# An entry of the experts' token lists becomes 64 bytes instead of 4

## The chip, the cores and the metric

The kernel runs on one core of one Trainium2 chip. The metric is the device time of one execution in microseconds, lower being better; the time shown for a kernel is the median of several executions. A core has five engines with a queue of instructions each: TensorE (PE in the profile; its weight loads are PEld), VectorE (DVE), ScalarE (ACT), GpSimd (POOL) and SyncE (SP, which only issues DMAs). POOL issues the indirect DMAs, whose rows are picked by a list of indices. An engine runs its queue in order: an instruction that waits holds up all behind it.

## The reference, cut to what matters

The model has two layers on x of shape (4, 512, 512), all in float32. The first is a cumulative cross-attention and a feed-forward layer with Hadamard transforms. The second is a softmax attention over 1024 context rows a batch, and then a mixture of experts, which is the stage in question:

```python
router_logits = x2d @ gate_kernel                       # 2048 tokens, 32 experts
routing_weights = softmax(router_logits)
routing_weights, selected_experts = top_k(routing_weights, 8)
routing_weights = routing_weights / sum(routing_weights)
...                                                     # the tokens of each expert, sorted
inter = silu(tokens @ gate_proj[e]) * (tokens @ up_proj[e])   # 512 -> 192
expert_out = inter @ down_proj[e]                             # 192 -> 512
output[token] = sum over its 8 experts of weight * expert_out
x = x + output
```

2048 tokens with 8 experts each make 16384 pairs of token and expert.

## The kernel before, in words

**Before the experts.** Up to 725 us of the profiled execution the kernel does the first layer and loads; from 725 to about 1055 us it goes over the 16 tiles of 128 tokens (loop `for step in range(NTT)`), and each step holds a stage of several tiles: scores, read-out, router (`choose`) and `place_rows`.

**The lists.** `il_d` is a list in DRAM: each expert has a stretch of LS = 2320 entries of one int32, an entry being a token's number. Entries never written hold a number past the last token, put there early by `blank_rows` (L120 to 134). `place_rows(t)` (L1063 to 1092) counts, on TensorE and DVE, which place in its experts' stretches each token of tile t gets, writes the eight places into `slots`, and then POOL issues eight indirect DMAs (L1082), one for each of a token's eight experts: 128 words of 4 bytes, each to its own place in `il_d`. There are 128 of these scatters.

**Early experts.** Six experts (EARLY) start on the tokens of the first 11 tiles. `start_early` (L1094) reads two column tiles of their lists at once; `early_rows` gathers their token rows into the wide buffers big2, big0, big1, big3 (experts 0 to 3) and two smaller tiles (4, 5); their steps are T (transposes), G (the products of gate and up) and D_ (down), put between the last steps of the attention by an order written out by hand for PE, DVE and ACT. D_ writes its results over the gathered rows, and `early_adds` has POOL add them to the output in DRAM.

**The loop over all experts.** After the lists are complete, the 32 experts are gone through by size ("rank"); their tile counts and tile heights are fixed (FIXED: 7 tiles of 126 tokens, six of 128, and so on to 2 of 100). An expert with more than four tiles is worked in two *parts*: 14 of the 32 are (one of 7 tiles, five of 6, eight of 5). The order is the three largest, then the largest left, each of the next five behind one of the small ones, so that among experts 0 to 31 of the loop numbers 3, 5, 7, 9 and 11 are small. For each expert:

- `load_list` (L1426): SP reads the expert's entries from `il_d` into `ids`, five experts ahead; eight `ids` tiles rotate. `read_lists` (L911) makes each such read wait for all scatters.
- `load_rows` (L1435): POOL gathers the token rows by these numbers, one DMA a tile (`gather`, L903), three experts ahead, into one of three `xg` tiles. It is called by `turned`, when the last part of the expert three before has been transposed; that expert's weight sums (`weights_of`, L1410), which read the same tile, must be done too.
- `turn` (L1346 and following): TensorE transposes the rows; ACT and DVE copy them out of PSUM (L1164, L1166).
- `gate_up` (L1361): three products on TensorE (L1373) through two PSUM tiles; ACT does the Silu of the first (L1173), DVE multiplies it with the second (L1174), and the third product, the rest of gate and up, goes into the first one's PSUM tile.
- `output` (L1447): `down` on TensorE (L1188, L1191); `finish` scales each result tile by the routing weight and writes it to `y`, even tiles on ACT (L1200), odd ones on DVE (L1198); then `add_rows` (L1384) has POOL issue one indirect DMA a tile that adds y's rows to the output in DRAM (L1387). `tc.issue_after(gathers[-1])` puts these adds behind the gathers traced last in POOL's queue. The adds of one expert wait until those of the expert before have landed, since both may add to the same token's row.

TensorE works ahead: the transposes of the next part stand between this part's gate-up and down. `y` has tag "y" in a pool of three buffers, taken in turn by each part.

A dynamic loop after that (L1548 and following) takes the tokens that a fixed size had no room for.

Of the kernel before, what the change touches and what calls it, by code (L numbers as in the profile page):

```python
# [9 lines left out]
F32 = mybir.dt.float32  # L10
I32 = mybir.dt.int32
# [7 lines left out]
P = 128  # L19
# [4 lines left out]
EARLY = 6  # L24
ER = 2
# [8 lines left out]
    + [(3, 128), (3, 117), (3, 108), (3, 100)] + [(2, 112), (2, 100)]  # L34
)
SPARE = 1024


def most_extra(tokens: int, experts: int) -> int:
# [9 lines left out]
def kernel(  # L49
# [26 lines left out]
    nc = tc.nc  # L76
    B, S, D = x.shape
# [3 lines left out]
    NT = B * S  # L81
# [5 lines left out]
    NX = most_extra(NT, E)  # L87

    LS = NT + 272
    IL = -(-(E * LS + P) // SPARE) * SPARE  # L90

    XW = D + E

# [10 lines left out]
    xn_d = dram.tile([NT + SPARE, XW], F32, name="xn_d")  # L104
    xa_d = dram.tile([CUT * P + P, XW], F32, name="xa_d")

    il_d = dram.tile([IL, 1], I32, name="il_d")

    xe_d = dram.tile([1, NX], I32, name="xe_d")
    xi_d = dram.tile([P, NX], I32, name="xi_d")  # L110
# [11 lines left out]
    def blank_rows():  # L122


        room = x_sb[:, NTT - TPB :, :].rearrange("p t d -> p (t d)")
        zeros = room[:, :XW]
        nc.gpsimd.memset(zeros, 0.0)
        fill = room[: IL // SPARE, SPARE : 2 * SPARE].bitcast(I32)
        nc.gpsimd.iota(fill, pattern=[[1, SPARE]], base=NT, channel_multiplier=0)
        for i in range(SPARE // P):  # L130
            rows = slice(NT + i * P, NT + (i + 1) * P)
            nc.sync.dma_start(out=xn_d[rows, :], in_=zeros)
        nc.sync.dma_start(out=xa_d[CUT * P :, :], in_=zeros)
        nc.sync.dma_start(out=il_d.rearrange("(p f) o -> p (f o)", f=SPARE), in_=fill)

    def load_x(b):
        return nc.sync.dma_start(
# [765 lines left out]
    def gather(xg, src, idx, rows):  # L903
        ins = nc.gpsimd.indirect_dma_start(  # L904
            out=xg,
            out_offset=None,
            in_=src[:, :],
            in_offset=bass.IndirectOffsetOnAxis(ap=idx, axis=0),
            bounds_check=rows - 1,
            oob_is_err=False,  # L910
        ).ins  # L911
        gathers.append(ins)
        return ins

    def read_lists(dst, src):
        ins = nc.sync.dma_start(out=dst, in_=src).ins
        for s in scatters:
            tc.add_manual_dep(
                ins, s.name,
                mybir.DependencyInfo(mybir.DependencyClass.Sync, mybir.DependencyReason.DATA),  # L920
                reason="lists written",
            )
# [13 lines left out]
    with tc.tile_pool(name="ctx2", bufs=1) as ctx2, tc.tile_pool(  # L936
# [127 lines left out]
        def place_rows(t):  # L1064

            nonlocal run
            sel = chosen.pop(t)
            ps = ps_o.tile([P, 512], F32, tag="o", name="o")
            nc.tensor.matmul(ps[:, :E], upper, sel, start=True, stop=False)
            nc.tensor.matmul(ps[:, :E], ones, run, start=False, stop=True)  # L1070
            nxt = aw.tile([P, E], F32, tag="run", name="run")
            nc.vector.tensor_add(nxt, run, sel)
            run = nxt

            val = aw.tile([P, E], F32, tag="val", name="val")
            nc.vector.tensor_mul(val, ps[:, :E], sel)
            slot1 = small.tile([P, K], F32, tag="slot1", name="slot1")
            nc.vector.max(slot1, val)
            nc.vector.tensor_scalar_add(slots[:, t * K : (t + 1) * K], slot1, -1.0)
            for k in range(K):  # L1080
                j = t * K + k
                ins = nc.gpsimd.indirect_dma_start(  # L1082
                    out=il_d[:, :],
                    out_offset=bass.IndirectOffsetOnAxis(ap=slots[:, j : j + 1], axis=0),
                    in_=tok[:, t : t + 1],
                    in_offset=None,
                    bounds_check=IL - 1,
                    oob_is_err=False,
                ).ins
                if scatters:  # L1090
                    tc.declare_no_dep(ins, group="rows", reason="rows of different pairs")
                tc.add_to_no_dep_group("rows", ins)
                scatters.append(ins)

        def start_early():

            nonlocal run
            ps = ps_o.tile([P, 512], F32, tag="o", name="o")
            nc.tensor.matmul(ps[:, :E], ones, run, start=True, stop=True)
            nxt = aw.tile([P, E], F32, tag="run", name="run")  # L1100
            nc.vector.tensor_tensor(nxt, ps[:, :E], early1, ALU.max)
            run = aw.tile([P, E], F32, tag="run", name="run")
            nc.vector.tensor_scalar_mul(run, nxt, 1.0 / P)
            ids = route_p.tile([P, EARLY, ER], I32, name="ids")
            read_lists(
                ids,
                il_d[: EARLY * LS, :]
                .rearrange("(e n) o -> e n o", n=LS)[:, : ER * P, :]
                .rearrange("e (p c) o -> p e (c o)", c=ER),
            )  # L1110
            near = route_p.tile([P, EARLY, ER], I32, name="near")
            nc.vector.tensor_scalar_min(near, ids, float(CUT * P))
            early.extend((ids[:, e, :], near[:, e, :]) for e in range(EARLY))
# [188 lines left out]
    with tc.tile_pool(name="rw", bufs=1, reuse_waits="tile") as rw, tc.tile_pool(  # L1302
# [81 lines left out]
        def add_rows(y, idx):  # L1384


            ins = nc.gpsimd.indirect_dma_start(  # L1387
                out=of[:, :],
                out_offset=bass.IndirectOffsetOnAxis(ap=idx, axis=0),
                in_=y,  # L1390
                in_offset=None,
                bounds_check=NT - 1,
                oob_is_err=False,
                compute_op=ALU.add,
            ).ins
            group = f"adds{len(adds)}"
            if adds[-1]:
                tc.declare_no_dep(ins, group=group, reason="rows of different tokens")
            tc.add_to_no_dep_group(group, ins)
            for s in adds[-2]:  # L1400
                tc.add_manual_dep(
                    ins, s.name,
                    mybir.DependencyInfo(
                        mybir.DependencyClass.Sync, mybir.DependencyReason.DATA
                    ),
                    reason="sums of the rows before",
                )
            adds[-1].append(ins)
# [11 lines left out]
        class Fixed:  # L1420
# [5 lines left out]
            def load_list(self):  # L1426
                nt, q = self.nt, self.q
                at = number(start_i, self.r, (E - 1) * LS)
                self.ids = er.tile([P, TM], I32, tag="ids", name="ids", bufs=8)
                read_lists(  # L1430
                    self.ids[:q, :nt],
                    il_d[bass.ds(at, nt * q), :].rearrange("(p c) o -> p (c o)", c=nt),
                )

            def load_rows(self):  # L1435
                nt, q = self.nt, self.q
                self.xg = er.tile([P, TM, XW], F32, tag="xg", name="xg")
                for c in range(nt):
                    gather(self.xg[:q, c, :], xn_d, self.ids[:q, c : c + 1], NT + SPARE)

            def load_weights(self):
                self.wt = fetch(number(order_i, self.r, E - 1))
# [4 lines left out]
        def output(x, t0, nt, h1, h2, w):  # L1447
            q = x.q
            ps = down(h1, h2, nt, q, x.wt[1], x.wt[2])
            y = er.tile([P, 4, D], F32, tag="y", name="y")  # L1450
            for i in range(nt):
                finish(i, ps[i][:q, :D], y[:q, i, :], w[:q, t0 + i : t0 + i + 1])
            with tc.issue_after(gathers[-1]):
                for i in range(nt):
                    add_rows(y[:q, i, :], x.ids[:q, t0 + i : t0 + i + 1])


        large, little = list(range(26)), [30, 28, 27, 26, 29]
# [89 lines left out]
        with tc.If(nx > 0):  # L1548
# [59 lines left out]
            with tc.For_i(0, nx, 1) as i:  # L1608
                one = bass.ds(i, 1)
                e_t = er.tile([1, 1], I32, tag="e_t", name="e_t", bufs=1)  # L1610
                nc.sync.dma_start(out=e_t, in_=xe_d[:, one])
                row = er.tile([P, 1], I32, tag="row", name="row", bufs=1)
                nc.sync.dma_start(out=row, in_=xi_d[:, one])
                hot_t = er.tile([P, E], F32, tag="hot", name="hot", bufs=1)
                nc.sync.dma_start(
                    out=hot_t, in_=hot_d[one, :].rearrange("o e -> (o e)").partition_broadcast(P)
                )
                ids = er.tile([P, 1], I32, tag="ids1", name="ids1", bufs=1)
                gather(ids, il_d, row, IL)
                e = nc.sync.value_load(e_t[0:1, 0:1], min_val=0, max_val=E - 1)  # L1620
                x = Fixed(0, 1, P)
                x.wt, x.ids = fetch(e), ids
                x.xg = er.tile([P, TM, XW], F32, tag="xg", name="xg")
                gather(x.xg[:, 0, :], xn_d, ids, NT + SPARE)
                hs = gate_up(x.wt[0], turn(x.xg, 0, 1, P), 1, P)
                output(x, 0, 1, *hs[:2], weights_of(x.xg, hot_t, 1, P))
                adds.append([])
# [70 lines left out]
```

## Time and profile before

| | us |
|---|---|
| median of 3 executions | 1713.23 (1712.88 to 1713.24) |
| profiled execution, device time | 1729.91 |
| its span, from first to last instruction | 1728.1 |
| PE busy in the span | 1653.4 |
| POOL busy in the span | 597.1 |
| adds of y on POOL, 141 | 224.7 |
| gathers of token rows on POOL, 141 | 151.5 |
| scatters into the lists on POOL, 128 | 126.5 |

The profile is of one execution. A row of the timeline gives the start in us from the span's start, the time it took, engine, line, operation, output and inputs by the program's names with shapes, a count, and in brackets how long the engine had been idle before it and what ended that. Lines are those of the kernel before. In the chain of waits a row is a start, a time and what the end of the program was waiting for then; "issue" is time in which nothing that the profile shows was waited for. A row for a stretch of time gives its length, the busy time of PE, PEld, DVE, ACT and POOL with their instruction counts, the granted TensorE clock (1.00 is full), the share of the DMA engines' time and what they moved in GB/s. A row of the costliest groups gives busy time, mean ns of one, and the idle time just before them.

### The profile page before, as it was taken

To read this page: it belongs to the slowest core of one execution; us is meant where nothing else is said; L and a number is where in the kernel's file an instruction comes from. 1 tells how busy PE (TensorE), PEld (TensorE's weight loads), DVE (VectorE), ACT (ScalarE), POOL (GpSimd) and SP (SyncE) were. 2 spreads that over 40 slices of the span, in tenths; PEclk is the share of its full clock that TensorE was granted. 3 is DMA by queue.
4 is the path that set the end of the run, shared out by engine and by line. 5 is a ranking of instruction groups with operands and counts; after the bars stand their busy time and mean duration, and the time that the engine had idled before them with its cause. 6 is when DMAs were issued, how large, how long until landed. Compare 5 with 4: busy or idle time off the path is not lost.

```text
span 1728.1 us, 17728 instructions
## 1 busy us (share of the span) xinstructions
PE 1653.4 (96%) x6050; PEld 1010.0 (58%) x6050; DVE 764.7 (44%) x1715; ACT 509.7 (29%) x854; POOL 597.1 (35%) x522
## 2 busy tenths in 40 slices
PE   7999999999999999999999968999999999999996
PEld 3685657776766777545545445555555666544443
DVE  4693457755785445444434325223222323232332
ACT  2510333322332111145656522222222222222221
POOL 1000120101000100103444555657565675456664
PEclk9999999999999999999999988999999999999998
DMA  9314110000000000354431236979677887668774
GB/s 346 125 49 122 49 63 27 1 1 1 1 1 5 20 0 1 123 197 113 100 87 51 58 51 111 242 128 208 153 158 165 201 181 161 146 174 185 180 158 64
DMA packets 92718, 181.76 MB, mean 105 GB/s; under 512 B 23906, under 2 KB 24546, under 8 KB 92625
## 3 DMA queue, kind: packets, MB, share of 16 engines
q0 software_dynamic: 40560, 73.04, 23.3%
q1 hardware_dynamic: 51198, 106.72, 19.6%
q8 instruction: 48, 0.79, 0.2%
q10 hardware_dynamic: 866, 0.85, 0.2%
q14 instruction: 46, 0.37, 0.1%
HBM read 132.38 MB, written 51.62 MB: 106 GB/s over the span
## 4 chain that ended last, share of the span: by engine, by line
PE 82%; issue 5%; DMA 4%; DVE 4%; POOL 2%; ACT 2%; ACTq 0%; POOLq 0%; DVEq 0%; SPq 0%
PE g L1373 19%; PE q L717 17%; PE dn L364 11%; PE dn L1188 6%; PE o L1018 6%; PE sc L988 6%; PE gu L342 5%; PE dn L1191 4%; PE tr L1354 3%; DMA out_dram<-y,ids 2%; POOL il_d L1082 2%; PE tr L167 1%; DMA x_sb<-in_cn_dram 1%; PE gu L332 1%; PE o L1038 1%
## 5 line engine op out<-in xcount | busy, mean ns | idle before, releaser
L1373 PE MATMUL g<-xgt,gu 128*128 128x360 f32 (+24 forms) x1104 | 346.0, 470 | 0.0
L1373 PEld LDWEIGHTS g<-xgt,gu 128*128 128x128 f32 x1104 | 204.9, 190 | 149.9 <-issue 77.4
L1387 POOL DMA_INDIRECT out_dram<-y,ids x141 | 224.7, 1593 | 107.6 <-issue 39.1
L364 PE MATMUL dn<-wdn,h 128*128 128x512 f32 x448 | 200.3, 593 | 0.0
L904 POOL DMA_INDIRECT xg<-xn_d,ids x141 | 151.5, 1074 | 129.7 <-issue 107.9
L1082 POOL DMA_INDIRECT il_d<-tok,slots x128 | 126.5, 988 | 197.7 <-DVE sel L1052 70.9
L717 PE MATMUL q<-big,s 128*128 128x256 f32 x768 | 173.6, 379 | 0.0
L717 PEld LDWEIGHTS q<-big,s 128*128 128x128 f32 x768 | 145.9, 190 | 19.8
L1188 PE MATMUL dn<-d,h 128*126 128x512 f32 (+8 forms) x306 | 150.0, 600 | 0.0
L364 PEld LDWEIGHTS dn<-wdn,h 128*128 128x128 f32 x448 | 84.1, 190 | 92.8 <-issue 91.6
L717 PE MATMUL q<-big,wgu 128*128 128x256 f32 x576 | 132.4, 379 | 0.0
L1174 DVE TENSOR_TENSOR h<-g,sg 128x256 f32<-128x256 f32 (+25 forms) x52 | 27.0, 519 | 222.4 <-PE g L1373 204.9
L717 PEld LDWEIGHTS q<-big,wgu 128*128 128x128 f32 x576 | 109.3, 190 | 25.7 <-issue 9.3
L342 PE MATMUL gu<-big,wgu 128*128 128x256 f32 x512 | 117.9, 388 | 3.3 <-ACT sg L349 3.3
L1018 PE MATMUL o<-big,pt 128*128 128x512 f32 x256 | 116.4, 603 | 3.8 <-issue 2.6
L988 PE MATMUL sc<-big,qt 128*128 128x512 f32 x256 | 114.1, 599 | 0.3 <-ACT qt L170 0.3
L342 PEld LDWEIGHTS gu<-big,wgu 128*128 128x128 f32 x512 | 98.4, 194 | 26.8 <-issue 7.6
L374 POOL TENSOR_TENSOR x_sb<-x_sb,y 128x512 f32<-128x512 f32 x16 | 19.9, 1271 | 258.3 <-DVE y L373 258.3
L278 POOL TENSOR_TENSOR x_sb<-x_sb,beta_t 128x512 f32<-128x512 f32 x16 | 23.7, 1504 | 235.2 <-ACT y L267 222.7
L1200 ACT ACTIVATE y<-dn,w 126x512 f32<-126x512 f32 (+8 forms) x82 | 56.3, 687 | 139.2 <-PE dn L1191 134.5
L731 ACT ACTIVATE sg<-q,wsu_t 128x256 f32<-128x256 f32 x96 | 45.4, 473 | 171.5 <-DVE q L753 84.0
L1354 PEld LDWEIGHTS tr<-ident,xg 126*128 126x128 f32 (+8 forms) x564 | 64.9, 142 | 53.3 <-issue 19.1
(244 smaller groups left out, 1969.7 us busy)
## 6 DMA issues: line engine op xcount, KB each, us to landing
gu<-in_w_gu_dram SPq DMA_DIRECT2D x38, 768.0 KB
big<-in_cn_dram SPq DMA_DIRECT2D x10, 1024.0 KB
d<-in_w_dn_dram SPq DMA_DIRECT2D x38, 256.0 KB
big<-in_ct_dram SPq DMA_DIRECT2D x8, 1024.0 KB
x_sb<-in_cn_dram SPq DMA_DIRECT2D x12, 512.0 KB
d<-in_w_dn_dram SPq DMA_DIRECT2D x38, 128.0 KB
xn_d<-xr SPq DMA_DIRECT2D x16, 272.0 KB
x_sb<-in_x_dram SPq DMA_DIRECT2D x4, 1024.0 KB
```

The source lines that it names most:

```text
L342: nc.tensor.matmul(ps[:, :n], wt[:, c, fs], xhs[b][:, c, cols], start=(c == 0), stop=(c == DC - 1),)
L364: nc.tensor.matmul(ps[:, :D], h[:, i * P : (i + 1) * P], wdn[:, fc, :], start=(fc == 0), stop=(fc == FC - 1),)
L717: nc.tensor.matmul(q[:, m * HS : (m + 1) * HS], w[:, m, k, :], x[:, k, :], start=(k == 0), stop=(k == 1),)
L904: ins = nc.gpsimd.indirect_dma_start(out=xg, out_offset=None, in_=src[:, :], in_offset=bass.IndirectOffsetOnAxis(ap=idx, axis=0), bounds_c ...
L988: nc.tensor.matmul(ps[:, bass.ts(h, M // 2)], qt[:, c, :], keys[b][h][:, c, :], start=(c == 0), stop=(c == DC - 1),)
L1018: nc.tensor.matmul(ps[:, :D], pt[:, c, :], values[b][c // (MC // 2)][:, c % (MC // 2), :], start=(c == 0), stop=(c == MC - 1),)
L1082: ins = nc.gpsimd.indirect_dma_start(out=il_d[:, :], out_offset=bass.IndirectOffsetOnAxis(ap=slots[:, j : j + 1], axis=0), in_=tok[:, t : ...
L1188: nc.tensor.matmul(p[:q, :D], h1[:, bass.ts(i, q)], d1, start=True, stop=False)
L1191: nc.tensor.matmul(p[:q, :D], h2[half, bass.ts(i, q)], d2[half, :], start=False, stop=True)
L1354: nc.tensor.transpose(ps[:, h * q : (h + 1) * q], xg[:q, t0 + h, c * P : (c + 1) * P], ident[:q, :q],)
L1373: nc.tensor.matmul(p[:, :n], gu[:, c, k * P : (k + 1) * P], xgt[:, c, :n], start=(c == 0), stop=(c == DC - 1),)
L1387: ins = nc.gpsimd.indirect_dma_start(out=of[:, :], out_offset=bass.IndirectOffsetOnAxis(ap=idx, axis=0), in_=y, in_offset=None, bounds_che ...
```

## The change

An entry of `il_d` becomes a row of LW = 16 int32 (64 bytes), all sixteen holding the token's number. The following comes with it:

- `blank_rows` fills a list sixteen times as large: an iota of 128x1024 instead of 73x1024, and ten DMAs of 512 KB instead of one of 292 KB.
- `place_rows` first spreads the tile's token numbers over 16 columns on DVE (`entry`, two buffers) and scatters from there.
- `start_early` reads whole entries into a tile of tag "h1", and DVE copies the first column of each to `ids`.
- `load_list` reads whole entries, so that an `ids` tile has 16 times the size; gathers and adds take the first column of an entry.
- `y` leaves its pool of three buffers and takes one of the wide buffers big2, big0, big1, which the attention and the early experts used before. Which of them is chosen by `len(adds) % 3`; `adds` grows by one with each expert, not with each part.

In all queues the order of the other instructions is the same as before; DVE has 17 copies more and SP nine DMAs more.

```diff
+LW = 16
...
     LS = NT + 272
-    IL = -(-(E * LS + P) // SPARE) * SPARE
+    BL = P * SPARE // LW
+    IL = -(-(E * LS + P) // BL) * BL
...
-    il_d = dram.tile([IL, 1], I32, name="il_d")
+    il_d = dram.tile([IL, LW], I32, name="il_d")
...
-        fill = room[: IL // SPARE, SPARE : 2 * SPARE].bitcast(I32)
-        nc.gpsimd.iota(fill, pattern=[[1, SPARE]], base=NT, channel_multiplier=0)
+        fill = room[:, SPARE : 2 * SPARE].bitcast(I32)
+        some = SPARE // P
+        nc.gpsimd.iota(
+            fill.rearrange("p (n f w) -> p n f w", f=some, w=LW),
+            pattern=[[0, SPARE // LW // some], [1, some], [0, LW]],
+            base=NT,
+            channel_multiplier=some,
+        )
...
-        nc.sync.dma_start(out=il_d.rearrange("(p f) o -> p (f o)", f=SPARE), in_=fill)
+        for i in range(IL // BL):
+            nc.sync.dma_start(
+                out=il_d[i * BL : (i + 1) * BL, :].rearrange("(p f) w -> p (f w)", p=P), in_=fill
+            )
...
+            entry = aw.tile([P, LW], I32, tag="entry", name="entry")
+            nc.vector.tensor_copy(entry, tok[:, t : t + 1].to_broadcast([P, LW]))
             for k in range(K):
                 j = t * K + k
                 ins = nc.gpsimd.indirect_dma_start(
                     out=il_d[:, :],
                     out_offset=bass.IndirectOffsetOnAxis(ap=slots[:, j : j + 1], axis=0),
-                    in_=tok[:, t : t + 1],
+                    in_=entry,
...
+            entries = ee.tile([P, ER * P], F32, tag="h1", name="h1").bitcast(I32)
+            entries = entries[:, : EARLY * ER * LW].rearrange("p (e v) -> p e v", e=EARLY)
+            read_lists(entries, ...)
             ids = route_p.tile([P, EARLY, ER], I32, name="ids")
-            read_lists(ids, ...)
+            nc.vector.tensor_copy(
+                ids, entries.rearrange("p e (c w) -> p e c w", w=LW)[:, :, :, 0]
             )
...
             def load_list(self):
                 nt, q = self.nt, self.q
                 at = number(start_i, self.r, (E - 1) * LS)
-                self.ids = er.tile([P, TM], I32, tag="ids", name="ids", bufs=8)
+                ids = er.tile([P, TM, LW], I32, tag="ids", name="ids", bufs=8)
                 read_lists(
-                    self.ids[:q, :nt],
-                    il_d[bass.ds(at, nt * q), :].rearrange("(p c) o -> p (c o)", c=nt),
-                )
+                    ids[:q, :nt, :].rearrange("p c w -> p (c w)"),
+                    il_d[bass.ds(at, nt * q), :].rearrange("(p c) w -> p (c w)", c=nt),
+                )
+                self.ids = ids
...
             ps = down(h1, h2, nt, q, x.wt[1], x.wt[2])
-            y = er.tile([P, 4, D], F32, tag="y", name="y")
+            i = (2, 0, 1)[len(adds) % 3]
+            y = big.tile([P, 4, D], F32, tag=f"big{i}", name=f"big{i}")
             for i in range(nt):
                 finish(i, ps[i][:q, :D], y[:q, i, :], w[:q, t0 + i : t0 + i + 1])
             with tc.issue_after(gathers[-1]):
                 for i in range(nt):
-                    add_rows(y[:q, i, :], x.ids[:q, t0 + i : t0 + i + 1])
+                    add_rows(y[:q, i, :], x.ids[:q, t0 + i, 0:1])
```

## The prediction

> **What bounds the kernel now.** I read the page first: part 1, then the costliest groups.
>
> ```profile
> PE 1653.4 (96%) x6050; PEld 1010.0 (58%) x6050; DVE 764.7 (44%) x1715; ACT 509.7 (29%) x854; POOL 597.1 (35%) x522
> ...
> L1387 POOL DMA_INDIRECT out_dram<-y,ids x141 | 224.7, 1593 | 107.6 <-issue 39.1
> L904 POOL DMA_INDIRECT xg<-xn_d,ids x141 | 151.5, 1074 | 129.7 <-issue 107.9
> L1082 POOL DMA_INDIRECT il_d<-tok,slots x128 | 126.5, 988 | 197.7 <-DVE sel L1052 70.9
> ```
>
> TensorE is busy 96% of the span, so any time it is made to wait is added to the end. POOL spends 224.7 + 151.5 us on the adds and gathers of the experts' loop (1105 to 1728); with the 0.30 us that its rows show between issues that is 461 of 623 us. The scatters that the change names are 126.5 us, before that loop.
>
> Next the chain of waits, where lists become rows, with the rows of TensorE and the stage windows behind it:
>
> ```profile
> 1071.89 7.15 DMA il_d<-tok,slots
> 1079.30 4.12 DMA ids<-il_d
> 1087.19 10.59 DMA xg<-xn_d,ids
> ```
>
> ```profile
> 1097.83 1.10 PE L1354 MATMUL tr<-ident,xg 126*128 126x126 f32 x4 [2.56 <-DMA xg<-xn_d,ids]
> ```
>
> ```profile
> 1095.00:1098.00 3.00, 0.45 (x3) 0.21 (x3) 0.73 (x1) 0.63 (x1) 2.39 (x3) 0.85 1.03 281
> 1098.00:1101.00 3.00, 3.00 (x9) 1.86 (x10) 0.55 (x1) 0.47 (x1) 2.00 (x2) 0.50 1.02 279
> 1101.00:1104.00 3.00, 3.00 (x9) 1.50 (x9) 0.55 (x1) 0.47 (x1) 2.00 (x2) 0.51 1.07 289
> 1104.00:1107.00 3.00, 3.00 (x11) 1.46 (x10) 0.75 (x1) 0.69 (x1) 1.82 (x2) 1.00 1.08 316
> ```
>
> The last scatter lands 7.15 us after its issue, the list read takes 4.12, the gather 10.59. All that TensorE sees of it is 2.56 us of waiting, and then a granted clock of 0.50 until 1104.
>
> Last the loop itself, on ScalarE and POOL. "y" is the expert's result; POOL adds its rows to the output.
>
> ```profile
> 1135.16 0.69 ACT L1200 ACTIVATE y<-dn,w 126x512 f32<-126x512 f32 x1 [3.48 <-PE dn L1191]
> ...
> 1225.39 0.69 ACT L1200 ACTIVATE y<-dn,w 120x512 f32<-120x512 f32 x1 [3.02 <-PE dn L1191]
> 1226.25 0.69 ACT L1200 ACTIVATE y<-dn,w 120x512 f32<-120x512 f32 x1 [0.17 <-PE dn L1191]
> 1228.69 0.44 ACT L1173 ACTIVATE sg<-g 128x324 f32<-128x324 f32 x1 [1.75 <-PE g L1373]
> ```
>
> ```profile
> 1119.39 1.56 POOL L1387 DMA_INDIRECT out_dram<-big,ids  x1 [0.31 <-issue]
> ...
> 1150.21 1.64 POOL L1387 DMA_INDIRECT out_dram<-y,ids  x1 [1.81 <-ACT y L1200]
> ...
> 1154.07 1.59 POOL L1387 DMA_INDIRECT out_dram<-y,ids  x1 [0.30 <-issue]
> ...
> 1225.65 1.60 POOL L1387 DMA_INDIRECT out_dram<-y,ids  x1 [0.30 <-issue]
> 1232.35 1.06 POOL L904 DMA_INDIRECT xg<-xn_d,ids  x1 [5.10 <-issue]
> ...
> 1244.14 1.62 POOL L1387 DMA_INDIRECT out_dram<-y,ids  x1 [0.30 <-issue]
> 1250.32 1.59 POOL L1387 DMA_INDIRECT out_dram<-y,ids  x1 [4.56 <-DMA out_dram<-y,ids]
> ```
>
> The second part of the first expert writes y at 1135.16; POOL issues the adds of its *first* part only at 1150.21 to 1154.07. POOL runs some 32 us behind here, and 8 to 15 us later on (y at 1225.39, adds from 1240.24). It costs nothing today, since y rotates through three buffers. An add issued last at 1244.14 frees the next expert's first add at 1250.32: 6.18 us; other such hops are 5.87 to 7.47.
>
> **The change, part by part.**
>
> *Scatter, list, gather.* The DMA count is the same (128 scatters, 32 + 1 list reads). No row shows a 64-byte scatter. Its issue lies between the 4-byte scatter's 988 ns and the 2176-byte gather's 1074, so at most +0.7 us for the last eight. The list read grows from 3.5 to 56 KB, +0.2 us at the 276 GB/s moved there. Landing: the quickest DMA hop of the whole chain is 3.47 us, so the 7.15 can lose 3.7 at most, and gain nothing at least. For TensorE the gain cannot exceed its 2.56 us of waiting plus half of the 6.8 us at half clock: −6. Ends +1 and −6; I take −1.5, nearer to nothing, because the gather's 10.59 us is spent at a DMA share of 1.03 to 1.08 and an earlier start meets the same weight loads.
>
> The Trainium skill (DMA: Bandwidth & Descriptors, Specifications) says that a transfer under 512 bytes makes the DMA engine read, modify and write. By that rule a 64-byte entry is as partial as a 4-byte word, and this term would be +1 instead of −1.5; no row here shows a 64-byte write.
>
> *Entry tiles.* 16 copies of 128x16 and one of 128x12 on DVE; the nearest rows (128x8 at 171 ns, 128x32 at 192) give 0.2 each, under a DVE that is 44% busy; only the last lies ahead of scatters on the chain, +0.2. Each waits for the scatters two token tiles back, 20 us or more earlier. The fill goes from one DMA of 292 KB to ten of 512 KB and an iota of the same 1024 columns (0.98 us, with 5.7 us idle behind it). At the 346 GB/s of slice 0 that is 15 us of DMA from 250 us on, and the five slices from 302 us move 1 GB/s; the room it reads is reloaded a batch later. Cost: nothing.
>
> *y moves to the three wide buffers.* This is the term that decides. Before, a *part* took the next of three buffers; now an *expert* does, and both its parts take the same one. 14 of the 32 experts have two parts. The second part's first ScalarE write of y must wait until the first part's adds have landed. Behind it in ScalarE's queue stands the next part's Silu (1228.69), which frees the PSUM tile that TensorE needs for the third of that part's three products. So TensorE waits.
>
> Slack: for the expert with y at 1225.39, the next part's products start at 1226.14 and take 6.81 us, the third from 1230.7. Two y writes (1.55), a Silu (0.44) and hand-overs (0.25) must be done by then: y may be 3.0 us late. With four-tile parts next it is about 5.5, with two-tile parts 1.4 to 2.1.
>
> Lateness: the trace's completion record gives when the first part's adds landed (issued last 1154.07, landed 1159.9; 1225.65, 1233.0), against the second part's y. In order of experts 0, 1, 2, 4, 6, 8, 10, 12 to 18, landed minus y is 24.8, 17.8, 8.6, 7.6, 7.0, 7.0, 12.0, 11.8, 7.0, 1.6, 3.2, 3.1, 3.6, 1.9 us.
>
> Carrying forward: expert 0's first part also waits, for the early expert whose wide buffer it takes (add issued 1119.39, landed 1124.4, y due 1118.2): 0.9 past its slack. Then expert 0 loses 24.8 − 0.9 − 3.7 = 20.1. That pushes TensorE 21 us, while POOL's backlog moves only by 6; so experts 1 and 2 fall inside their slack: 0. From expert 4 on POOL has caught up. Its gathers are released by TensorE's work (1232.35 follows the loop's weight sums) and the adds queue behind them, so they shift with TensorE and the lateness recurs. Taking off slack, and up to 0.7 where y shifted a little more than the adds: 4.3, 3.0, 2.6 (experts 4, 6, 8), 8.7 and 8.6 (10, 12). Expert 13's falls to 2.9 after that: 1.0. Experts 14 to 17, with each y pushing the next adds a little: 0.2, 2.0, 2.2, 2.9. Expert 18 is followed by a four-tile part: 0. Sum 0.9 + 20.1 + 9.9 + 17.3 + 1.0 + 7.3 = 56.5.
>
> Ends: with every add landing 6.3 us after its issue, the same steps give 49; with 5.7, 40; with 10% longer landings than recorded, 70. I take 56.5 less 6: the stretched loop moves the same bytes in 10% more time, and hops are shorter where the traffic is thinner (6.34 at 1676, against 6.96 and 7.47 at 1283 and 1358); 5% shorter landings are worth 6.
>
> *The clock.* 2.56 us of idling cost 0.45 + 1.5 + 1.5 = 3.4 us of granted clock above; 1.5 us of idling before 1041.6 were followed by 0.51 over 1042.5 to 1046, 1.7 us. Nine of the stalls are of 2 us or more: 9 × 1.7 = 15. About half returns, since slower products before the next y make it less late: +8; ends 0 and 17.
>
> The Trainium skill (TensorE: Matmul & The Clock Gate, Part 1) has the clock halved after an idle window of about 3.4 us. The 2.56 and 1.5 us above did it already. By the rule only the four stalls over 3.4 us would be charged, 4 × 1.7 = 7, and after the half that returns +3 instead of +8.
>
> **Sum.** 56.5 − 6 + 8 − 1.5 = +57 us. The profiled execution took 1729.9 (span 1728.1 and 1.8 around it), 16.7 above the median of 1713.2; the timed executions run the same program, so I put the difference on the median: 1770.
>
> **Rivals.** (a) *Only the start pays.* Landings without a profiler, or thinned, are 20% shorter or more; then the recurring stalls mostly shrink into the slack and expert 0's 15 to 20 remain with a few of the others: +20 to +34, 1733 to 1747. For it: experts 14 to 18 are within 2 us of their slack. Against it: 10 and 12 are 12 us late.
> (b) *Faster: the 4-byte scatters cause the slow stretch before the loop.* From 983 to 1104 TensorE is busy 95.2 of 121 us and the windows show half clock for much of it; idle time and lost clock come to 26 + 17 = 43 us. If whole entries removed all of it and the stalls stayed under that, the kernel would be faster; with 5.7 us landings and no clock term, 40 − 43 = −3, 1710. It decides once the stretch gives back more than the stalls take. Against it: PE rows there wait for other things, and part of the stretch may belong to the profiled execution, which is 16.7 us longer than the timed ones.
> (c) *Worse.* Longer landings (70) with the whole clock term (17): +87, up to 1800.
> (d) *The waits do not bind*, because y's release comes earlier than I read: −6 to +1 from the lists alone, 1707 to 1714.
>
> **How the numbers follow.** The forecast's own range, 1747 to 1792, takes the ends 40 and 62 (7.0 us landings), the lists' −6 to 0 and the clock to 17: 0.68. Rival (a) 0.17, (c) 0.09, (b) 0.04, (d) 0.02. The range 1735 to 1798 leaves out (b), (d) and the outer part of (a) and (c). About 0.2% is what a measurement of this kernel tells from no change: faster 0.04, within 0.01, slower 0.95.
>
> **What would show it.** ScalarE's y writes of second parts, released by DMA out_dram; TensorE idle about 20 us in the first expert's neighbour (1142 to 1162) and 8 to 9 at two more; windows of half clock behind them; the last scatter's hop near 7 us still. I am wrong if y shows no wait for adds, or if adds land under 5 us.

## The result

The changed kernel takes 1763.1 us (median of 6 runs, 1759.0 to 1764.2), the kernel before 1713.2 (6 runs beside them): a ratio of 1.0284, 95% interval 1.0271 to 1.0298, +50 us. The forecast was 1770 (+57), range 1735 to 1798. Its sign and its place hold; its size does so in part by luck, since the experiments below show +50 to be a loss of about 67 and a gain of about 17, and of the gain the prediction had only 1.5.

One thing has to be known for the traces that follow. On some chips every profile, of either entry size, has pauses about 1010 and 1055 in which VectorE and ScalarE wait for something that the records don't name; TensorE stands idle 6 to 11 us at the first and mostly 1 to 6 us at the second. In these profiles 24 to 34% of the records of landing DMAs are missing too, in the others under 1%. The profile of before in the prediction (1729.9 us, where the timed runs take 1713.2) has them; the profile of after (1763.0) has not.

The page of after, two of its costliest groups (busy, mean ns | idle before them, and what ended it), and TensorE's row:

```profile
PE 1658.3 (94%) x6050; PEld 1009.7 (57%) x6050; DVE 766.3 (44%) x1732; ACT 506.7 (29%) x854; POOL 598.2 (34%) x522
...
L1392 PE MATMUL g<-xgt,gu 128*128 128x360 f32 (+24 forms) x1104 | 358.6, 481 | 47.6 <-ACT sg L1192 47.6
...
L1219 ACT ACTIVATE big<-dn,w 126x512 f32<-126x512 f32 (+8 forms) x82 | 54.7, 686 | 232.1 <-DMA out_dram<-big,ids 119.4
```

The g products, which never waited before, now wait 47.6 us in all for ScalarE's Silu (the tile sg). ScalarE in turn waited 119.4 us for adds to out_dram to land before it could write y (now a wide buffer, "big"). The timeline of after on ScalarE, on POOL and on TensorE (start, duration, engine, line; in brackets the wait before it and what ended it):

```profile
1129.10 1.59 POOL L1406 DMA_INDIRECT out_dram<-big,ids  x1 [0.30 <-issue]
...
1135.17 1.27 ACT L1219 ACTIVATE big<-dn,w 126x512 f32<-126x512 f32 x2 [26.45 <-DMA out_dram<-big,ids]
1136.33 0.49 ACT L1192 ACTIVATE sg<-g 128x384 f32<-128x384 f32 x1
...
1136.87 5.49 PE L1392 MATMUL g<-xgt,gu 128*128 128x384 f32 x8 [18.49 <-ACT sg L1192]
```

The last add of the first expert's first part is issued at 1129.10 and lands at 1135.07, 5.97 us later. The second part's y is written at 1135.17, the Silu queued behind it runs at 1136.33, and TensorE goes on at 1136.87 after 18.49 us. One hop follows on the other, as the prediction had it. It also shows the recurring case, here the expert with loop number 10 (POOL, ScalarE, TensorE):

```profile
1340.40 1.13 POOL L916 DMA_INDIRECT xg<-xn_d,ids  x1 [0.30 <-issue]
...
1346.00 1.07 POOL L916 DMA_INDIRECT xg<-xn_d,ids  x1 [0.30 <-issue]
1347.37 1.65 POOL L1406 DMA_INDIRECT out_dram<-big,ids  x1 [0.30 <-issue]
1349.32 1.61 POOL L1406 DMA_INDIRECT out_dram<-big,ids  x1 [0.30 <-issue]
...
1357.74 1.27 ACT L1219 ACTIVATE big<-dn,w 126x512 f32<-126x512 f32 x2 [14.42 <-DMA out_dram<-big,ids]
...
1359.37 4.37 PE L1392 MATMUL g<-xgt,gu 128*128 128x300 f32 x8 [8.32 <-ACT sg L1192]
```

Five gathers stand in POOL's queue in front of the two adds; the second add lands at 1357.63, y follows, and TensorE has waited 8.32 us. All the waits for Silu, by the part that the predicted one belongs to (us):

| expert (loop number) | 0, first part | 0 | 1, 2 | 4 | 6 | 8 | 10 | 12 | 13 | 14 | 15 | 16 | 17 | sum |
|---|---|---|---|---|---|---|---|---|---|---|---|---|---|---|
| predicted | 0.9 | 20.1 | 0 | 4.3 | 3.0 | 2.6 | 8.7 | 8.6 | 1.0 | 0.2 | 2.0 | 2.2 | 2.9 | 56.5, less 6 |
| after | 2.97 | 18.49 | 0.22 | 3.51 | 0.85 | 0.50 | 8.32 | 7.61 | 1.43 | 1.59 | 1.64 | 0.18 | 0.26 | 47.6 |

The lists, last: DMA issues of after by kind (KB each, median us from issue to landing).

```profile
il_d<-entry,slots POOLq DMA_INDIRECT x128, 2.1
big<-xa_d,near POOLq DMA_INDIRECT x8, 3.7
```

Before, the last scatter's hop was 7.15 us; here a scatter lands after 2.1 us, and the last one after 2.12. The first gather of the experts' loop is issued at 1059.3, against 1084.3 in the profile of before. How much of those 25 us is the entries and how much the pauses, the two profiles cannot say; in two later profiles without pauses, of one chip, it is issued at 1071.5 with words (the kernel before) and at 1059.4 with 64-byte entries (y by part, below), so about 12 go with the entries.

### The profile page after: what moved, and what is told of

Its sections match the earlier page's. It is cut to its first block, busy times and chain, and to the rows that moved or that the text cites. A ratio compares the mean times of both kernels' runs of the same rounds, so it can differ in the third digit from the quotient of the medians.

```text
span 1761.3 us, 17768 instructions
## 1 busy us (share of the span) xinstructions
PE 1658.3 (94%) x6050; PEld 1009.7 (57%) x6050; DVE 766.3 (44%) x1732; ACT 506.7 (29%) x854; POOL 598.2 (34%) x522
## 3 DMA queue, kind: packets, MB, share of 16 engines
q0 software_dynamic: 40560, 74.02, 22.1%
## 5 line engine op out<-in xcount | busy, mean ns | idle before, releaser
L1392 PE MATMUL g<-xgt,gu 128*128 128x360 f32 (+24 forms) x1104 | 358.6, 481 | 47.6 <-ACT sg L1192 47.6
L1406 POOL DMA_INDIRECT out_dram<-big,ids x149 | 237.7, 1595 | 150.5 <-ACT big L1219 73.6
L1096 POOL DMA_INDIRECT il_d<-entry,slots x128 | 126.5, 989 | 181.3 <-DVE sel L1064 137.6
L1217 DVE TENSOR_SCALAR big<-dn,w 126x512 f32<-126x512 f32 (+8 forms) x59 | 44.2, 750 | 202.3 <-DMA out_dram<-big,ids 116.6
L1219 ACT ACTIVATE big<-dn,w 126x512 f32<-126x512 f32 (+8 forms) x82 | 54.7, 686 | 232.1 <-DMA out_dram<-big,ids 119.4
```

What stands on the lines that cost most here:

```text
L1096: ins = nc.gpsimd.indirect_dma_start(out=il_d[:, :], out_offset=bass.IndirectOffsetOnAxis(ap=slots[:, j : j + 1], axis=0), in_=entry, in_o ...
L1219: nc.scalar.activation(y, ps, AF.Copy, scale=weight)
L1392: nc.tensor.matmul(p[:, :n], gu[:, c, k * P : (k + 1) * P], xgt[:, c, :n], start=(c == 0), stop=(c == DC - 1),)
L1406: ins = nc.gpsimd.indirect_dma_start(out=of[:, :], out_offset=bass.IndirectOffsetOnAxis(ap=idx, axis=0), in_=y, in_offset=None, bounds_che ...
```

## The experiments

Four came first, together on one chip. It turned out to be one with pauses: before took 1727.3 us there.

**y by part.** All of the change stays, but y takes the next wide buffer with each part, three in turn, as its buffers of before did:

```
+        part_no = iter(range(99))
         def output(x, t0, nt, h1, h2, w):
-            i = (2, 0, 1)[len(adds) % 3]
+            i = (2, 0, 1)[next(part_no) % 3]
```

> The 64-byte entries stay; y takes the next of the three wide buffers with every part instead of every expert. Theory (the second part's wait for its first part's adds is the whole loss): the 47.6 us that TensorE's g products wait for ScalarE's Silu go, and the lower clock behind them; what is left is the list term of the prediction, -1.5 us (ends -6 and +1), so 1711.7, between 1707 and 1714.5. Rival 1 (the 4-byte scatters cause the slow stretch before the loop in every execution): the profile of after has 2.2 us of long idling there where before has 24.6, so about 22 us under before, 1691. Rival 2 (the wide buffers or the larger lists cost time in themselves): over 1725.

Measured: 1730.4 us against 1727.3, ratio 1.0002, interval 0.9978 to 1.0027. Its group of g products shows 0.0 us of idling. So the second part's wait is the whole loss; no gain of the entries can be seen here.

**y alone.** The opposite: 4-byte words as before, y moved as in after.

```
-            y = er.tile([P, 4, D], F32, tag="y", name="y")
+            i = (2, 0, 1)[len(adds) % 3]
+            y = big.tile([P, 4, D], F32, tag=f"big{i}", name=f"big{i}")
```

> The 4-byte words stay; only y moves to the wide buffers, one per expert. Theory: the loss is all here. Waits of the g products for Silu of 45 to 57 us, about 20 of them at the first expert, and 1758 to 1772 us, as after plus the little that the entries gain. Rival (the 64-byte entries share in the loss, by longer list reads or DMA traffic): clearly under after, 1740 or less.

Measured: 1788.0 us, ratio to before 1.0363, interval 1.0337 to 1.0389: +61, and 57.6 over the kernel with y by part on the same chip. The expectation in us was written for a chip where before takes 1713; against before, +45 to +59 was expected, and +61 is just over it. Its table of waits, for TensorE's g products (us in total, times, longest):

```profile
PE g L1373 <- ACT sg L1173: 43.7, 12, 18.1
```

and the longest of them on TensorE's timeline, the first expert's:

```profile
1162.29 4.27 PE L1373 MATMUL g<-xgt,gu 128*128 128x384 f32 x8 [18.09 <-ACT sg L1173]
```

43.7 us of waiting, just under the 45 expected, 18.09 of it at the first expert. TensorE's busy time is 1662.7 against 1654.7 us with y by part: 8.0 us of lower clock. The 64-byte entries have no share in the loss.

**The first expert apart.** As after, but the second part of the first expert alone has another buffer:

```
-            i = (2, 0, 1)[len(adds) % 3]
+            n = len(adds) + 2 * (x is work[0] and t0 > 0)
+            i = (2, 0, 1)[n % 3]
```

> As after, but the second part of the first expert alone takes another buffer. The first expert's 18.5 us wait goes. Theory (the backlog of adds on POOL is what is waited for, and only moves): the next expert's second part is now late by about the 17.8 us of the record of before, 14 after its slack, so a stall of 11 to 16 us shows one expert later and only 2 to 7 us are gained: 1756 to 1761. Rival (each stall stands for itself): 18.5 us and some 2 us of clock are gained, 1741 to 1745.

It ran here (1781.1 us, ratio 1.0313, interval 1.0289 to 1.0337) and again beside after, on a chip without pauses where before took 1715.7 us:

> The same kernel as e3_first_expert_apart, now beside after on one chip. It had 13.2 us of waiting at the second expert in place of 18.5 at the first, and 43.0 in all against 47.6. Theory (the backlog moves): 2 to 7 us under after. Rival (each stall stands for itself): 18 to 21 us under.

Measured there: 1759.1 us, and after itself 1766.8: 7.7 us gained (10.5 us less waiting in the two profiles), somewhat over the 2 to 7 of the theory and far from 18 to 21. TensorE's timeline of the second run has its longest wait here:

```profile
1156.57 4.94 PE L1392 MATMUL g<-xgt,gu 128*128 128x360 f32 x8 [11.58 <-ACT sg L1192]
```

and its page gives the group of the g products:

```profile
L1392 PE MATMUL g<-xgt,gu 128*128 128x360 f32 (+24 forms) x1104 | 358.3, 481 | 42.4 <-ACT sg L1192 42.4
```

The first expert's 16 to 18 us are gone, and 11.58 us stand one expert later, where after waited under 0.5. The long wait is a backlog of adds on POOL that the first expert who needs a buffer back pays for.

**A word in an entry of its own.** As y by part, but a scatter writes 4 bytes into its 64-byte entry:

```
-                    out=il_d[:, :],
+                    out=il_d.rearrange("n w -> (n w)").unsqueeze(1),
...
-                    in_=entry,
+                    in_=tok[:, t : t + 1],
```

(and the slots are multiplied by LW).

> As e1_y_by_part, but each scatter writes only the first 4 bytes of its own 64-byte entry (the rest of the entry is never read). If it is the neighbours in a shared line that make a 4-byte scatter slow, these scatters land 2 to 3 us after issue as the whole entries do (2.1 us); if it is the partial write, they land after 3 to 8 us and grow through the last eight, as in before. In time both differ by at most the few us of the list term: within 4 us of e1_y_by_part.

Measured: ratio 1.0007, interval 0.9988 to 1.0027. By the completion record of the trace, in which about 30% of the completions are missing on this chip, the scatters land after 2.06 us in the median, and after 3.87 at most among the last 24; with whole entries 2.04 and 3.96; with 4-byte words beside each other (y alone, same chip) 5.7 and 16.5. So it is not the partial write that makes a word slow, but how close the words lie; why closeness costs, no run shows.

**After again.**

> The changed kernel itself, on a chip where the kernel before and the experiments can stand beside it. Theory: 43 to 50 us of waiting of the g products for Silu and 5 to 8 us of lower clock, and a list term of 0 to -4: 48 to 58 us over before on this chip. In the first three experiments before took 1727, its profiled runs had 9 to 11 and 4 to 6 us of idling about 1010 and 1055 that neither part of the change removed; the profile of after has none of it. If the entries removed it, after has none of it here either, and the distance to before is under 40.

Measured: 1766.8 us against 1715.7, ratio 1.0293, interval 1.0270 to 1.0317: +51. The waits for Silu are 52.9 us. The distance is within the 48 to 58 of the theory (the waits are 2.9 over its 50). The pauses are missing here, and the distance is still 51, so the other reading, that the entries remove them, does not fit: the pauses go with the chip (each was used once), not with the entries.

**Adds ahead of gathers.** As after, but the rows of the third expert ahead are gathered behind the adds of the part before. The call of load_rows moves out of turned():

```
             output(x, t0, nt, h1, h2, w)
+            if i + 1 < len(parts):
+                with tc.issue_after(adds[-1][-1]):
+                    next_rows(*parts[i + 1])
```

> As after (y one buffer per expert), but POOL issues the gathers of the third expert ahead behind the adds of the part before instead of in front of them. Theory (the recurring waits are made of five gathers of 1.4 us each, or three, that stand in POOL's queue in front of the first part's adds): lateness at the experts 10 and 12 falls by 6.9 us and at 4, 6, 8 by 4.1, to under or about the slack of 3; their waits of 8.3, 7.6, 3.5, 0.9, 0.5 fall to 3 at most in each; the first expert's 18 us, which comes from the early experts' adds, stays within 4. Waits for Silu 18 to 28 in all, 20 to 30 us under after. Rival (the landing of the adds alone makes them late, the gathers are in nobody's way): 43 to 48 us of waiting as in after, and the same time within 5 us.

Measured: 1731.2 us, 35.6 under after on the same chip; before's ratio 1.0093, interval 1.0072 to 1.0114. The group of the g products on its page:

```profile
L1392 PE MATMUL g<-xgt,gu 128*128 128x360 f32 (+24 forms) x1104 | 352.5, 476 | 27.4 <-ACT sg L1192 27.4
```

and the longest wait that is left, on TensorE's timeline:

```profile
1136.46 5.49 PE L1392 MATMUL g<-xgt,gu 128*128 128x384 f32 x8 [18.36 <-ACT sg L1192]
```

27.4 us of waiting are left of 52.9, of which 5.76 and 18.36 are at the first expert's two parts; no wait at the experts 4 to 10 is over 0.5 us. That is 25.5 us less waiting, and TensorE's busy time falls from 1658.4 to 1648.1 us: 10.3 us of clock come back with it. The sum, 35.8, is what was measured. So the gathers in front of the adds were the recurring waits, and the expectation left out the clock.

**Entries of 32 bytes** (LW = 8, y by part) ran once on the same chip:

> As e1_y_by_part with entries of 32 bytes, written whole, two to each 64 bytes. If it is neighbours within 64 bytes that slow the landing, the scatters land later than the 2 to 2.9 us (4.8 at most among the last eight) of 64-byte entries, some at 3 to 6 us; if 4-byte neighbours alone do it, 2 to 3 us as with 64. Time: within 5 us of before on the chip either way.

Measured: 1696.3 us in one run, where before took 1715.7, and landings as with 64 bytes (2.1 us in the median, 4.85 at most among the last eight). The 19 us were unexpected: the prediction had 6 at most. This opened the question of what the entries give where nothing pauses.

**Before, profiled, and y by part again**, together on another chip without pauses.

> The kernel before itself, for a profile of it beside e10 on one chip. Two kinds of executions have been seen: with pauses of 9 to 11 and 4 to 6 us about 1010 and 1055 in which VectorE and ScalarE wait for something that the records don't name (the profile of before, and all four of the first experiments, 64-byte entries or not), and without (the later ones, 64- and 32-byte entries, where before took 1715.7). Theory (the pauses belong to the chip or to the loaded program, not to the scatters): where e10 has them, before has them too. Rival (the 4-byte scatters bring the pauses, or others as long): before has them where e10 has none.

> The kernel of e1_y_by_part (64-byte entries, y by part) on another chip. e8_entries_of_32_bytes took 1696.3 once where before took 1715.7. Theory (the entries gain only the list term): where there are pauses, 0 +- 4 us against before as in e1_y_by_part; where there are none, -1.5 to -6. Rival (the entries free the stretch before the loop of 4-byte traffic, and pauses on the chip of the first experiments hid that): where there are none, 15 to 22 us faster than before, ratio 0.987 to 0.991, and 65 to 73 us under after, of which 53 are waits and 12 to 20 clock.

Measured: before 1716.4 us, y by part 1699.6, ratio 0.9902, interval 0.9885 to 0.9919: 16.8 us faster than before, and the fastest version that was timed in several runs. Neither has a pause. The new profile of before shows TensorE's waits between 1000 and 1100, which the profile in the prediction could not show:

```profile
PE tr L1210 <- DMA xg<-xa_d,near: 8.2, 2, 5.1
...
PE tr L1354 <- DMA xg<-xn_d,ids: 4.5, 2, 2.9
```

Its DMA issues from 1000 to 1065, by kind (count, median us from issue to landing):

```profile
il_d<-tok,slots POOLq DMA_INDIRECT x32, 11.5
xg<-xa_d,near POOLq DMA_INDIRECT x4, 13.1
```

And its windows (length, busy time of PE, PEld, DVE, ACT and POOL, then granted clock, DMA share, GB/s):

```profile
1054.00:1057.00 3.00, 0.38 (x1) 0.18 (x1) 0.00 (x0) 0.00 (x0) 1.39 (x2) 0.77 0.07 11
1057.00:1060.00 3.00, 0.07 (x1) 0.00 (x0) 0.00 (x0) 0.00 (x0) 1.51 (x2) 0.50 0.02 0
1060.00:1063.00 3.00, 2.86 (x8) 2.21 (x9) 0.00 (x0) 0.76 (x2) 2.33 (x2) 0.50 0.07 6
...
1040.00:1100.00 60.00, 47.30 (x170) 29.63 (x171) 21.18 (x46) 9.70 (x20) 37.84 (x34) 0.86 0.82 189
```

In this stretch a 4-byte scatter lands 11.5 us after its issue. The near-row gathers of an early expert, issued among the scatters on the same queue, take 13.1, and TensorE waits 8.2 us for them; the lists' own rows cost 4.5 more. From 1054 to 1063 TensorE did 3.31 us of work while the DMA share was 0.07, 0.02 and 0.07: at the end of its wait hardly any bytes were moving. Before that it is the other way round: from 1000 to 1054 the DMA share is 0.80 for 119 GB/s, with y by part and 64-byte entries 0.41 for 130 GB/s. The scatters' own packets are short in both (14 and 32 ns in the mean), but the 4352-byte packets of the row gathers beside them take 522 ns with words and 253 with entries. The same DMA issues of y by part with 64-byte entries on that chip:

```profile
il_d<-entry,slots POOLq DMA_INDIRECT x34, 2.4
...
xg<-xa_d,near POOLq DMA_INDIRECT x4, 4.5
```

and the same window:

```profile
1040.00:1100.00 60.00, 60.00 (x234) 36.16 (x233) 30.05 (x56) 12.99 (x27) 42.18 (x36) 1.00 0.80 215
```

Landings of 2.4 and 4.5 us, TensorE without a pause from 1040 to 1100, at a clock of 1.00 instead of 0.86. The 12.7 us of waiting and the 4.2 us by which its busy time is shorter (1645.0 against 1649.2) make 16.9, and 16.8 were measured in the medians. That the two agree so well is chance: the two profiled executions are only 14.5 us apart, since y by part idles 4.3 us more before 980 in its one. In the loop, from 1100 to 1400, TensorE is busy 298.44 of 300 us with before and 298.27 with y by part, so the gain is not from the buffers of y but lies ahead of the loop.

**Two more on the entries** ran on one chip; it had pauses again (before 1729.0 us).

> The kernel of e4 (y by part; 4 bytes written into an entry of 64 bytes of its own) where there may be no pauses. There its scatters landed after 2 to 2.9 us, as whole entries do. Theory (it is the neighbours that made the words slow, not that they are partial): as e10, 14 to 19 us faster than before where there are no pauses (ratio 0.989 to 0.992). Rival (only whole entries gain): within 5 us of before.

> As e10 with entries of 16 bytes, written whole, four to each 64 bytes. 32-byte entries landed after 2.1 to 2.4 us among the last five and gave 1696.3. If what slows the landing is neighbours within 64 bytes, four of them are slower than two: landings of 3 to 8 us and less than half the gain; if it needs closer neighbours than 16 bytes, landings of 2 to 3 us and the whole gain, 14 to 20 us under before where there are no pauses.

Measured: the word in its own entry 0.9949 (0.9926 to 0.9972), 16-byte entries 1.0012 (0.9989 to 1.0035). Both land after 2.04 us in the median and 3.60 and 3.94 at most among the last 24. So, by the two thirds of the completions that are recorded, 16 bytes between neighbours are enough for the landing. In time these two runs settle nothing, since the pauses cover the stretch in question; the word's 0.9949 also differs from its 1.0007 on the first chip, which stays unexplained. What a word in its own entry or a 16-byte entry is worth without pauses was not measured.

What a pause looks like, in the first run of y by part (VectorE, then TensorE):

```profile
1012.95 0.19 DVE L1054 COPY lg<-o 128x32 f32<-128x32 f32 x1 [12.99 <-remote]
...
1019.05 0.69 PE L1229 MATMUL tr<-ident,big 128*128 128x128 f32 x2 [11.39 <-ACT xgt L1185]
```

VectorE waits 12.99 us for a releaser outside the record ("remote") and TensorE 11.39 behind it. The profile of before had the same about 1010: "PE L1210 MATMUL tr<-ident,big" after 9.57 us that ended with "issue".

## Why the prediction was right, and where it was wrong

*The second part's wait for its first part's adds* was right, in mechanism and size: 50.5 us predicted, 47.6 and 52.9 in the two profiles of after, and 0 once y goes by part. The split was right too: 18.49 and 16.50 at the first expert (20.1 predicted), about 8 at the experts 10 and 12. Two details of the carrying forward were off: experts 6 and 8 waited 1.35 us together instead of 5.6, and 16 and 17 0.44 instead of 5.1. The backlog of adds on POOL and the gathers in front of them, given as causes, were each shown by a run.

*The clock* was too small: +8 predicted, and 13.4 us measured (busy time 1658.4 in the second run of after, 1645.0 with y by part, both without pauses, on two chips; the 8.0 of y alone against y by part is from a chip with pauses, which cost clock in both). It lies within the ends of 0 and 17. The step that is not borne out is "About half returns". Two windows of after (columns as above), behind the 8.32 us wait and behind a wait of 1.59:

```profile
1362.00:1365.00 3.00, 3.00 (x10) 1.93 (x9) 0.74 (x3) 0.78 (x2) 2.19 (x2) 0.65 0.62 146
1453.00:1456.00 3.00, 2.46 (x15) 2.35 (x16) 1.57 (x5) 1.04 (x4) 2.69 (x2) 1.00 0.29 29
```

The clock is 0.65 after the long wait, and 1.00 after the short one. The clock record of after has half clock for 5.4 us behind the first expert's wait, 4.7 and 5.2 behind the two of about 8 us, and 3.4 behind those of 2.97 and 3.51: 22.1 us, half of them lost, 11.0; the same in its second run is 27.0 us, 13.5 lost. So five stalls paid and not nine, the long ones 2.4 us and more instead of 1.7, and the whole price, 11 to 13.5, is near the 15 of the prediction. What was to return are shorter waits; they were 47.6 and 52.9 us against 56.5 less 6, so none is seen, though no run separates it.

Which waits pay is not told by their length alone. In after, those of 2.18 us (at 1009) and 2.97 (at 1101) did and those of 1.43 to 1.64 did not; in its second run 2.19 (at 1006), 2.67 and 2.69 did not. In these records the granted clock changes only at the edges of steps of 3.41 us. Over all fourteen traces, without their first 60 us and last 20, 87 steps at full clock have TensorE idle for 2.02 us or more, and half clock follows every one; of 6469 with less than 1.45 it follows 3, and of the 37 between, 11. A wait that lies across an edge is split: the 2.67 us are 0.86 in one step and 1.81 in the next. The rule that the prediction weighed (Trainium skill, TensorE: Matmul & The Clock Gate, Part 1: an idle window of about 3.4 us) would have given +3 against 13.4 measured; waits of 2.18 and 2.97 us, under that figure, were enough here.

*Scatter, list, gather* was wrong: −1.5 predicted with ends of −6 and +1, and −16.8 measured. Two sentences failed. "Landing: the quickest DMA hop of the whole chain is 3.47 us, so the 7.15 can lose 3.7 at most" took a floor from other transfers; the hop went to 2.12. "For TensorE the gain cannot exceed its 2.56 us of waiting plus half of the 6.8 us at half clock" took a bound from an execution that paused. In it the waits of TensorE for near rows, 8.2 us without pauses, do not occur; that the pauses gave those rows time to land is the likeliest reading, but no run tested it by itself. The difference of 16.7 us between that profile and the timed runs was seen, but "the timed executions run the same program, so I put the difference on the median" treated it as a constant. The rule that was weighed here (Trainium skill, DMA: Bandwidth & Descriptors, Specifications: under 512 bytes the engine reads, modifies and writes) gave +1 and was farther off. 64, 32 and 16 bytes, and 4 bytes in an entry of their own, all land in about 2.1 us; only words side by side took 5.7 in the median and up to 16.

*Entry tiles and fill* cost nothing, as predicted: between 240 and 720 us, where the ten fills run, TensorE is busy 479.35 of 480 us with y by part and 480.00 with before.

*The sum* was +57 and the measurement +50 because two errors of opposite sign met, which is luck: the list term 15 too little gained, and the clock and the waits together some 8 too little lost. Over the chips without pauses the ratios 1.0293 and 0.9902 put y's move at 1.0395, +67 us on 1699.6, against 58.5 predicted for waits and clock.

*The rivals.* (a) Only the start pays: no, 26 to 32 us of the waits come later. (b) The 4-byte scatters cause the slow stretch: half right. They cost 17 us there in runs without pauses, not 43, and the stalls outweigh that four times; the idle time that it was argued from was mostly pauses (9.57, 4.00 and 5.81 of 26 us). (c) Longer landings: no, the adds of y land after 5.8 us in the median in after and 5.7 in the new profile of before; the last ones of the first parts took 5.8 to 9.0. (d) The waits do not bind: no. Of the signs named ahead, "the last scatter's hop near 7 us still" was wrong (2.12); the others came as written, the long idle time some 24 us earlier than the window named.

## What to carry to other kernels

A buffer that rotates by a coarser unit than the work that fills it makes the work wait for its own output; count the buffers per fill, not per object, and look at which queue empties them. Before a bound is read from a profile, set its time beside the timed runs: where it is 1% longer, find the excess in the timeline first, since it may have covered the very wait that the change removes. And a scatter of 4-byte words into neighbouring places can be slow itself and hold up the transfers beside it: spreading the words by 16 to 64 bytes brought the landing here from 5.7 to 2.1 us, and with 64 bytes 16.8 us of 1716 in time when the buffer for y was put right.

## What was not expected of the hardware

- Neighbouring 4-byte words, written by scatters at once, land 11.5 us after issue in the median of the last 32, and while they do the DMA share is 0.80 for 119 GB/s (0.41 for 130 with entries), falling to 0.02 to 0.07 at the end; 4 bytes in entries 64 bytes apart land after 2.06.
- Half clock follows where TensorE was idle for 2.02 us or more of one 3.41 us step of the clock record, 87 times of 87, so a wait of 2.2 us can pay and one of 2.7 not.
- The pauses about 1010 and 1055 came on the chips of six runs and were missing in the other six, with 4-, 32- and 64-byte entries among these, and with 4-, 16- and 64-byte ones among those. What VectorE and ScalarE wait for in them stays open; where they come, they cover the whole gain of the entries in y by part (1.0002).
